# Softmax denominators of an attention layer: from a product with ones on TensorE to transpositions and sums on VectorE

## The chip, the cores and the metric

The kernel runs on one core of a Trainium2 chip. The metric is the time of one execution on the device in microseconds (us). A core has engines that run side by side, each with its own instruction queue, worked off in order: TensorE (PE in the profile; PEld is its weight load), VectorE (DVE), ScalarE (ACT), GpSimd (POOL) and SyncE (SP), which here issues most of the DMAs. They wait for one another through semaphores.

## What is computed

Four layers on a 512 x 64 x 64 image x, each of the form x = x + f(groupnorm(x)). Only the first one, an attention over the 4096 pixels, is touched:

```python
q, k, v = to_tokens(conv1x1(x, wq)), to_tokens(conv1x1(x, wk)), to_tokens(conv1x1(x, wv))
AA = jnp.sum(q * q, axis=-1)
sim = -(AA[:, :, None] + AA[:, None, :] - 2.0 * qk) * scale   # the key's norm is that of q
attn = jax.nn.softmax(sim, axis=-1)
out = jnp.einsum('bij,bjd->bid', attn, v)                     # 8 heads of 64
return conv1x1(out, wo)
```

Everything is float32. The softmax over the keys needs, for each query and head, the sum of the exponentials over all 4096 keys. That sum, its reciprocal and the multiplication with it are the subject of the change.

## The kernel before

The attention (`_attention_pairs`, lines 548 to 935) works on pairs of heads, 4 pairs, and for each pair on 8 blocks of 512 queries. x, K, V, and O stay in SBUF; the list QO holds Q of a pair and, after the division, its output O, in the same place.

For each pair, `project` (line 680) computes Q and K, and for pairs 0 and 2 also V of two pairs, by Strassen-Winograd's scheme of seven products p1 to p7 instead of eight. VectorE makes differences of X (tiles diff, line 463) and sums of weights (w_sum, line 450), TensorE makes the products (lines 467 and 535), and ScalarE and VectorE take them out of PSUM (kept, lines 509, 513, 740, 758, 760). The products are made in the order p1, p5, p2, p7, p6, p3, p4. The weights for the pair come by SyncE (line 696) and are scaled on GpSimd (line 404).

Then the blocks. A block has 32 steps t of 128 keys. In step t TensorE makes the scores of 128 keys and 512 queries for both heads (line 822, four products on quarters of 64 x 64 of its array), ScalarE takes the exponential (line 830, tile pt, 128 x 1024: keys on partitions, two heads of 512 queries side by side), and, two steps later, TensorE multiplies with V (line 842, two accumulators av in PSUM) and VectorE adds pt into acc (line 909). There are five pt buffers. At the end of a block, acc holds for each query 128 partial sums, one in each partition; they are still to be added over the partitions. The two av are added into avs (lines 914 and 919).

`close` (line 849) does the rest for a block, three steps into the next block (`t == AHEAD + 1`): two products with a matrix of ones sum acc over the partitions, and leave each sum on all 64 partitions of its head; VectorE inverts it (512 columns on 128 partitions), multiplies avs with it and makes two steps of a running check, `good`, that all sums lie within limits. A PSUM buffer is taken for it from the three that the scores use (tag "s"):

```python
for h in range(2):
    nc.tensor.matmul(ps[h * D : (h + 1) * D, :], ones, acc[:, ts(h, BLK)], start=True, stop=True)
rd = p3.tile([P, BLK], FP, tag="row", name="rd")
nc.vector.reciprocal(rd, ps)
nc.vector.tensor_mul(QO[pair][:, ts(b, BLK)], av, rd)
```

Of the 32 closings, 28 lie inside a block; those of block 7 of pairs 0 to 2 lie in the next pair's projection, after p5; the last lies among the last output products. In pair 3, `output` (line 864) follows each block from the second on: four chunks of four products with wo (line 869), added to X (line 873), with statistics for the next layer (line 877). At the end `good` is reduced to one number, okay, which every engine loads (line 947) for a branch (line 948): if a sum were out of its limits, a general version of the attention would run instead.

A scheduler orders the instructions of each engine by what they depend on and by the program's order; what is marked with `keep_in_program_order` stays in that order, the rest may move.

Of the kernel before, what the change touches and what calls it, by code (L numbers as in the profile page):

```python
# [10 lines left out]
FP = mybir.dt.float32  # L11
# [150 lines left out]
@with_exitstack  # L162
def trunk_kernel(ctx: ExitStack, tc: tile.TileContext, a: dict, out: bass.AP):
    nc = tc.nc

    base = ctx.enter_context(tc.tile_pool(name="base", bufs=1))
    small = ctx.enter_context(tc.tile_pool(name="small", bufs=1))


    X = base.tile([P, NC, N], FP, tag="X", name="X")  # L170
    def load_x(chunks, engines):
        for b in range(NB):
            for c, eng in zip(chunks, engines):
                eng.dma_start(out=X[:, c, ts(b, BLK)], in_=a["x"][c, :, ts(b, BLK)])

    load_x((0, 1), (nc.sync, nc.scalar))

    vec = base.tile([P, NVEC], FP, tag="vec", name="vec")
    nc.gpsimd.dma_start(out=vec, in_=a["vecs"])

    def vcol(name, i):
        at, n = _VEC_AT[name]
        return vec[:, at + i : at + i + 1]

    def vall(name):
        at, n = _VEC_AT[name]
        return vec[:, at : at + n]

    ident = base.tile([P, P], FP, tag="ident", name="ident")
    make_identity(nc, ident)  # L190

    gmask = base.tile([P, P], FP, tag="gmask", name="gmask")
    nc.gpsimd.memset(gmask, 1.0 / GROUP)
    for cm, step, first in ((1, -GROUP, 0), (-1, GROUP, GROUP - 1)):
        nc.gpsimd.affine_select(
            out=gmask,
            in_=gmask,
            compare_op=ALU.is_ge,
            fill=0.0,
            base=first,  # L200
            pattern=[[step, P // GROUP], [0, GROUP]],
            channel_multiplier=cm,
        )

    neg2 = base.tile([D, 1], FP, tag="neg2", name="neg2")
    nc.vector.memset(neg2, -2.0)

    def new_stats():
        return small.tile([P, NC, NB, 6], FP, tag="stats", name="stats")

    centered = _Centered(tc, small)

    dram = ctx.enter_context(tc.tile_pool(name="dram", bufs=1, space=bass.MemoryType.DRAM))
    F = [dram.tile([P, FORM.planes, FORM.plane], FP, tag=f"F{i}", name=f"F{i}") for i in range(NDW)]
    F3 = [
        dram.tile([P, FORM3.planes, FORM3.plane], FP, tag=f"G{i}", name=f"G{i}")
        for i in range(NQKV)
    ]
    Z = dram.tile([NB, BLK], FP, tag="Z", name="Z")

    stats, mv = _attention(
        tc, a, X, ident, gmask, neg2, small, new_stats, centered,
        lambda: load_x((2, 3), (nc.sync, nc.sync)),
    )

    stats, norm = _gated_convs(tc, a, X, vcol, vall, gmask, small, new_stats, centered, stats, mv, F)
    _linear_attention(tc, a, X, vcol, vall, ident, gmask, small, centered, stats, norm, F3, Z, out)

# [316 lines left out]
SUM_LOW, SUM_HIGH = 1e-20, 1e30  # L545


def _attention_pairs(tc, a, X, QO, gmask, small, centered, stats, mv, okay, load_rest):

# [16 lines left out]
    with tc.tile_pool(name="att1", bufs=1) as p1, tc.tile_pool(  # L568
# [95 lines left out]
        nc.vector.memset(halves, 0.0)  # L664
        nc.vector.memset(halves[0:D, 0:1], -2.0)
        nc.vector.memset(halves[D:P, 1:2], -2.0)
        ones = p1.tile([P, D], FP, tag="ones", name="ones")
        nc.vector.memset(ones, 1.0)
        good = p1.tile([P, BLK], FP, tag="good", name="good")
        nc.vector.memset(good, 1.0)  # L670
        K = p1.tile([P, N], FP, tag="K", name="K")
        V = p1.tile([P, N], FP, tag="V", name="V")
# [4 lines left out]

            return V if pair % 2 else QO[NC - 1]

        def project(pair, meanwhile=None):  # L680


            if pair == 0:
# [78 lines left out]
            late, psa = [], []  # L762
            if pair == 0:
                taken(1, 0, NC)
            pieces = differences(0)
            for k in range(NB // 2):
                after = iter(())
                for g, (wa, wb, ws, sums) in enumerate(made):
                    values = g + 1 < len(made)
                    dst = [home(pair), home(pair + 1)] if values else [Q, K]  # L770
                    steps = (turned if values else seven).steps(
                        wa, wb, ws, diff, view(k), bank, keep,
                        lambda m, n, ps, more: put(dst[m], 2 * k + n, ps, more),
                        p1_kept=begun.get((k, values)) if pair == 0 else None,
                    )
                    for n, step in enumerate(steps):
                        if n == 0:
                            next(sums, None)
                            next(pieces, None)
                            next(pieces, None)  # L780
                        if n == 1:
                            _all(sums)
                            _all(pieces)
                        step()
                        if n == 1 and meanwhile:
                            meanwhile()
                            meanwhile = None
                        if n == 3 and late:
                            late.pop()()
                        if not values and n == 2 and k + 1 < NB // 2:  # L790
                            pieces = differences(k + 1)
                        for _ in range(0 if values else {2: 2, 5: 4}.get(n, 0)):
                            next(pieces, None)
                if not psa:
                    psa.append(ps_s.tile([P, 2 * BLK], FP, tag="s", name="ps_a"))
                sq = ptp.tile([P, 2 * BLK], FP, tag="pt", name="sq")
                for n in range(2):
                    nc.scalar.activation(
                        sq[:, ts(n, BLK)], Q[:, ts(2 * k + n, BLK)], AF.Square
                    )  # L800
                late.append(lambda k=k, sq=sq: squares(k, sq))
# [44 lines left out]
                        start=(t == 0), stop=(t == NT - 1),  # L846
                    )

        def close(pair, b, av, acc):

            ps = ps_mm.tile([P, BLK], FP, tag="mm", name="ps_d")
            for h in range(2):
                nc.tensor.matmul(
                    ps[h * D : (h + 1) * D, :], ones, acc[:, ts(h, BLK)], start=True, stop=True
                )
            rd = p3.tile([P, BLK], FP, tag="row", name="rd")
            nc.vector.reciprocal(rd, ps)
            nc.vector.tensor_mul(QO[pair][:, ts(b, BLK)], av, rd)
            nc.vector.scalar_tensor_tensor(
                good, rd, 1.0 / SUM_HIGH, good, ALU.is_ge, ALU.mult  # L860
            )
            nc.vector.scalar_tensor_tensor(good, rd, 1.0 / SUM_LOW, good, ALU.is_le, ALU.mult)

        def output(b, chunks):
            cols = ts(b, BLK)
            for o in chunks:
# [4 lines left out]
                    )  # L871
                xs = X[:, o, cols]
                add = nc.vector.scalar_tensor_tensor(xs, ps, gain_out, xs, ALU.mult, ALU.add)
                if (b, o) == (NB - 1, 0):
                    past(mybir.EngineType.PE, mm)
                    past(mybir.EngineType.Pool, nc.gpsimd.memset(none, 0.0))
# [2 lines left out]
                    _aggregate(nc, mv, stats, o)  # L879

        for pair in range(HEADS // 2):
            project(pair, pair and (lambda: close(*done)))
            if pair == HEADS // 2 - 1:

                w = p1.tile([P, 3, NC, P], FP, tag="wqkv", name="wo")
                wo = [w[:, i] for i in range(3)] + [p1.tile([P, NC, P], FP, tag="wo", name="wo")]
                for o in range(NC):
                    ins = nc.sync.dma_start(out=wo[o], in_=a["L0_wo"][:, :, ts(o, P)])
                past(mybir.EngineType.SP, ins)
            done = None  # L890
            for b in range(NB):
                av = [
# [1 line left out]
                ]  # L894
                acc = p2.tile([P, 2 * BLK], FP, tag="acc", name="acc")
                pts = {}
                for t in range(NT + AHEAD):
                    if t < NT:
                        pts[t] = scores(pair, b, t)
                    if t == AHEAD + 1 and done is not None:  # L900
                        close(*done)
                    if t >= AHEAD:
                        u = t - AHEAD
                        pt = pts.pop(u)
# [16 lines left out]
                if pair == HEADS // 2 - 1 and 0 < b < NB - 1:  # L921
                    output(b - 1, range(NC))
            if pair == HEADS // 2 - 1:
                output(NB - 2, range(2))
                close(*done)
        output(NB - 2, range(2, NC))
        output(NB - 1, range(NC))


        one = p1.tile([P, 1], FP, tag="one", name="one")  # L930
        nc.vector.tensor_reduce(one, good, AX.X, ALU.min)
        ps = ps_mm.tile([P, BLK], FP, tag="mm", name="ps_ok")
        nc.tensor.matmul(ps[0:1, 0:1], one, ones[:, 0:1], start=True, stop=True)
        nc.vector.tensor_scalar(okay, ps[0:1, 0:1], float(P), None, ALU.is_ge)


def _attention(tc, a, X, ident, gmask, neg2, small, new_stats, centered, load_rest):

    nc = tc.nc
    gain_out = 1.0 / math.sqrt(C)  # L940
# [2 lines left out]
    okay = small.tile([1, 1], mybir.dt.int32, tag="okay", name="okay")  # L943
    stats = new_stats()
    mv = small.tile([P, NC, 2], FP, tag="mv", name="mv")
    _attention_pairs(tc, a, X, O, gmask, small, centered, stats, mv, okay, load_rest)
    found = nc.values_load(okay[0:1, 0:1])
    with tc.If(found < 1, label="general"):

# [1254 lines left out]
```

## Time and profile before

| What | Value |
|---|---|
| time, median of 3 runs | 3821.49 us (3817.75 to 3822.82) |
| the profiled execution's own time | 3822.72 us |
| its span in the profile | 3821.0 us |
| granted TensorE clock, mean | 0.996 |
| attention, first scores to last output product | 128.6 to 2243.4 us |
| weight loads (PEld) | 1658.8 us (43%) |
| the longest item by line on GpSimd and DMA | none near the span: GpSimd 4% busy, DMA about 1 GB/s for most of attention |

A busy time counts each moment once in which an engine works. Matmul records overlap each other, so the mean length of one (0.59 us) is longer than the pace at which they follow: eight of 64*64, four at a time, follow each other at 0.86 us. A float32 product appears as two records. In a line of groups, the numbers after the bar are busy time in us and the mean of one in ns; after the second bar is the idle time of the engine ahead of these instructions and what ended it. Idle time of VectorE behind ScalarE, and of ScalarE behind TensorE, means that TensorE sets the pace.

In the list of waits, the places where an engine waits for closing's results are few: weight loads for the scores wait 10.9 us in 28 times for rd, and one ScalarE copy in a projection waits 9.0 us for the multiplication with it.

### The profile page before, as it was taken

Reading aid. Unit: us, or ns where it says so; the run is one execution under the profiler, and the core shown is the slowest. Engines: PE = TensorE matmul, PEld = TensorE weight load, DVE = VectorE, ACT = ScalarE, POOL = GpSimd, SP = SyncE. Lnnn points to the kernel's source line nnn. Section 1 sums busy time; section 2 is a strip of 40 time slices with the busy share of each in tenths; the row PEclk is TensorE's granted clock in tenths of the full one; section 3 lists DMA queues with packets and bytes.
Section 4 is the critical chain, followed back from the end, with each engine's and each line's share of the span. In section 5 each row is a group of like instructions: output and inputs, shape, how many; then the busy total and the mean of one; then the engine's idle time right before and its main releaser. Section 6 shows DMA issues by size and latency. Waiting matters only on the chain. (4 is left out here: it accounts for less than half of the span.)

```text
span 3821.0 us, 81661 instructions
## 1 busy us (share of the span) xinstructions
PE 3753.6 (98%) x35298; PEld 1658.8 (43%) x35298; DVE 2693.8 (70%) x3261; ACT 2063.6 (54%) x2989; POOL 138.5 (4%) x117
## 2 busy tenths in 40 slices
PE   7999999999999999999999999999999999999999
PEld 5633334333364333343333334554444544455543
DVE  6677777777765777776766757766677677665537
ACT  2577774777735777746665645663246632354210
POOL 1000000000000000000000000000000000122122
PEclk9999999999999999999999999999999999999999
DMA  2000000000000000000000015772056730463312
GB/s 100 9 1 1 1 1 9 1 1 1 1 1 9 1 1 1 1 9 1 1 1 1 1 50 174 195 202 77 13 158 194 201 100 27 150 183 100 97 56 91
DMA packets 178414, 212.92 MB, mean 56 GB/s; under 512 B 13032, under 2 KB 121832, under 8 KB 177920
## 3 DMA queue, kind: packets, MB, share of 16 engines
q1 hardware_dynamic: 152384, 150.56, 14.3%
q10 hardware_dynamic: 25632, 57.01, 4.1%
q8 instruction: 280, 4.59, 0.5%
q14 instruction: 86, 0.70, 0.1%
q0 software_dynamic: 32, 0.06, 0.0%
HBM read 147.81 MB, written 59.77 MB: 54 GB/s over the span
## 5 line engine op out<-in xcount | busy, mean ns | idle before, releaser
L830 ACT ACTIVATE pt<-ps_s,A 128x512 f32<-128x512 f32 x2048 | 1286.2, 687 | 534.8 <-PE ps_s L822 527.2
L909 DVE TENSOR_TENSOR acc<-acc,pt 128x1024 f32<-128x1024 f32 x960 | 1174.3, 1223 | 327.9 <-ACT pt L830 301.8
L822 PE MATMUL ps_s<-O,K 64*64 64x512 f32 x8192 | 1111.7, 589 | 0.0
L822 PEld LDWEIGHTS ps_s<-O,K 64*64 64x64 f32 x8192 | 334.5, 133 | 553.3 <-issue 307.0
L842 PE MATMUL av<-pt,O 64*64 64x512 f32 x4096 | 558.3, 590 | 0.9 <-ACT pt L830 0.9
L842 PE MATMUL av<-pt,V 64*64 64x512 f32 x4096 | 554.4, 590 | 0.0
L1083 ACT COPY S<-S 32x1295 f32<-32x1295 f32 (+1 forms) x272 | 341.4, 1256 | 212.8 <-DMA S<-F 107.4
L842 PEld LDWEIGHTS av<-pt,O 64*64 64x64 f32 x4096 | 171.6, 133 | 275.8 <-issue 254.5
L842 PEld LDWEIGHTS av<-pt,V 64*64 64x64 f32 x4096 | 168.3, 133 | 281.0 <-issue 270.3
L1010 PE MATMUL ps<-diff,w_sum 128*128 128x512 f32 x516 | 241.9, 601 | 3.7 <-DVE w_sum L450 2.3
L1010 PEld LDWEIGHTS ps_cv<-S,T 64*32 64x32 f32 x13824 | 193.5, 105 | 110.4 <-issue 73.2
L1010 PE MATMUL ps_cv<-S,T 64*32 64x128 f32 x13824 | 232.4, 273 | 4.8 <-DVE turned L1137 1.6
L1010 PE MATMUL ps<-h,w_out_L 128*128 128x512 f32 x512 | 229.6, 599 | 1.5 <-DVE X L1364 1.4
L463 DVE TENSOR_TENSOR diff<-X 128x512 f32<-128x512 f32 x200 | 133.8, 686 | 72.1 <-PE ps L1010 46.2
L1010 PE MATMUL ps<-X,w_in_L 128*128 128x512 f32 x304 | 148.2, 620 | 11.0 <-ACT kept L1286 5.5
L391 ACT ACTIVATE X<-X,gn_less 128x512 f32<-128x512 f32 x118 | 74.5, 709 | 153.2 <-DVE gn_less L127 153.2
L1010 PE MATMUL ps<-h,pw_L 128*128 128x512 f32 x320 | 144.9, 602 | 2.6 <-DVE h L1352 2.3
L1010 PEld LDWEIGHTS ps<-diff,w_sum 128*128 128x128 f32 x516 | 94.6, 190 | 117.2 <-issue 107.3
L1010 PEld LDWEIGHTS ps<-h,w_out_L 128*128 128x128 f32 x512 | 94.0, 190 | 118.3 <-issue 96.5
L463 DVE TENSOR_TENSOR diff<-X,diff 128x512 f32<-128x512 f32 x200 | 135.2, 686 | 12.8 <-PE ps L1010 11.3
L1137 DVE STREAM_TRANSPOSE h<-ps_cv 128x512 f32<-128x512 f32 x112 | 109.4, 1051 | 48.2 <-PE ps_cv L1010 47.9
L1010 PE MATMUL ps<-agg,w_proj 128*128 128x512 f32 x256 | 118.4, 602 | 0.0
(239 smaller groups left out, 3336.1 us busy)
## 6 DMA issues: line engine op xcount, KB each, us to landing
T<-in_L_T_dram SPq DMA_DIRECT2D x112, 384.0 KB, 4.2
F<-plane ACTq DMA_DIRECT2D x112, 324.0 KB, 3.8
S<-F SPq DMA_DIRECT2D x224, 162.0 KB, 4.7
S<-G SPq DMA_DIRECT2D x96, 153.0 KB, 4.2
G<-plane ACTq DMA_DIRECT2D x48, 289.0 KB, 2.4
row<-G SPq DMA_DIRECT2D x48, 272.0 KB, 3.4
T<-in_L_T_dram SPq DMA_DIRECT2D x48, 256.0 KB, 3.9
out_dram<-y SPq DMA_DIRECT2D x32, 256.0 KB, 2.0
```

The source lines that it names most:

```text
L391: return self.nc.scalar.activation(xs, xs, AF.Identity, bias=less)
L463: yield eng.tensor_tensor(t[j][c], a(c), b(c), ALU.subtract)
L822: nc.tensor.matmul(ps[ts(half, D), ts(h, BLK)], K[rows, t * P + half * D : t * P + (half + 1) * D], QO[pair][rows, cols], start=True, stop ...
L830: exp = nc.scalar.activation(pt[:, ts(h, BLK)], ps[:, ts(h, BLK)], AF.Exp, bias=A[:, t, h : h + 1])
L842: nc.tensor.matmul(av[half][rows, :], v[keys, t * P + h * D : t * P + (h + 1) * D], pt[keys, ts(h, BLK)], start=(t == 0), stop=(t == NT - 1),)
L909: add = nc.vector.tensor_add(acc, acc if u > 1 else first, pt)
L1010: self.tc.keep_in_program_order(self.nc.tensor.matmul(*args, **kw))
L1083: nc.scalar.copy(second, first)
L1137: nc.vector.transpose(out, src)
```

## The change

`close` is replaced by `closing`, which gives four pieces to be put at chosen places: turn, partial, whole and divide. The sum over the partitions is made by VectorE: acc is transposed in 32x32 blocks in place (turn); each row of 32 is summed, from 128x1024 to 128x32 (partial); the four groups of 32 partitions are brought together by three copies and summed, the 1024 sums, now 32x32, are inverted and transposed back, written to a DRAM tile R, and read back twice, each time one head's 512 values onto 64 partitions (whole); then avs is multiplied (divide). The check `good` shrinks to 32x32. In a block, the pieces stand at steps 3, 6, 9 and 20; in a projection, after its first, second, third and seventh product; at the end, the first three before the outputs of block 6, and the division before the last chunk of these. The reciprocals' tile rd leaves the pool that it shared with kept and avs. The sums of weights of pairs 1 to 3 are listed ahead of the projection. The hint for the branch on SyncE moves from the wo loads to the last but one closing. The last product, ps_ok, becomes a transposition and sums.

```diff
-        def close(pair, b, av, acc):
-
-            ps = ps_mm.tile([P, BLK], FP, tag="mm", name="ps_d")
-            for h in range(2):
-                nc.tensor.matmul(
-                    ps[h * D : (h + 1) * D, :], ones, acc[:, ts(h, BLK)], start=True, stop=True
-                )
-            rd = p3.tile([P, BLK], FP, tag="row", name="rd")
-            nc.vector.reciprocal(rd, ps)
-            nc.vector.tensor_mul(QO[pair][:, ts(b, BLK)], av, rd)
...
+        def closing(pair, b, avs, acc):
+
+            within = b < NB - 1 or pair == HEADS // 2 - 1
+            pin = tc.keep_in_program_order if within else lambda ins: ins
+            rd = p1.tile([P, BLK], FP, tag="rd", name="rd")
+            one, recip = (rd[0:32, P + 32 * i : P + 32 * (i + 1)] for i in range(2))
+
+            def turn():
+                pin(nc.vector.transpose(acc, acc))
+
+            def partial():
+                pin(
+                    nc.vector.tensor_reduce(
+                        rd[:, 0:32], acc.rearrange("p (t k) -> p t k", k=32), AX.X, ALU.add
+                    )
+                )
+
+            def whole():
+                for q in range(1, P // 32):
+                    pin(
+                        nc.vector.tensor_copy(rd[0:32, ts(q, 32)], rd[ts(q, 32), 0:32])
+                    )
+                nc.vector.tensor_reduce(
+                    one, rd[0:32, 0:P].rearrange("p (q t) -> p t q", t=32), AX.X, ALU.add
+                )
+                nc.vector.reciprocal(one, one)
+                nc.vector.transpose(recip, one)
+                nc.sync.dma_start(out=R, in_=recip)
+                nc.vector.scalar_tensor_tensor(
+                    good, one, 1.0 / SUM_HIGH, good, ALU.is_ge, ALU.mult
+                )
+                nc.vector.scalar_tensor_tensor(
+                    good, one, 1.0 / SUM_LOW, good, ALU.is_le, ALU.mult
+                )
+                for h in range(2):
+                    ins = nc.sync.dma_start(
+                        out=rd[ts(h, D), :],
+                        in_=bass.AP(R.tensor, R.offset + h * BLK, [[0, D], [1, BLK]]),
+                    )
+                if (pair, b) == (HEADS // 2 - 1, NB - 2):
+                    past(mybir.EngineType.SP, ins)
+
+            def divide():
+                pin(
+                    nc.vector.tensor_mul(QO[pair][:, ts(b, BLK)], avs, rd)
+                )
+
+            return [turn, partial, whole, divide]
```

Where the pieces are put, in the projection, in the blocks and at the end:

```diff
             late, psa = [], []
             if pair == 0:
                 taken(1, 0, NC)
+            else:
+                _all(made[0][3])
...
-                        if n == 1 and meanwhile:
-                            meanwhile()
-                            meanwhile = None
+                        if meanwhile and n in (0, 1, 2, 6):
+                            meanwhile.pop(0)()
...
+                pieces = dict(zip((3, 6, 9, 20), closing(*done) if done else ()))
                 for t in range(NT + AHEAD):
                     if t < NT:
                         pts[t] = scores(pair, b, t)
-                    if t == AHEAD + 1 and done is not None:
-                        close(*done)
+                    if t in pieces:
+                        pieces[t]()
...
             if pair == HEADS // 2 - 1:
-                output(NB - 2, range(2))
-                close(*done)
-        output(NB - 2, range(2, NC))
+                pieces = closing(*done)
+                for piece in pieces[:3]:
+                    piece()
+                output(NB - 2, range(NC - 1))
+                pieces[3]()
+                output(NB - 2, range(NC - 1, NC))
         output(NB - 1, range(NC))
...
-        one = p1.tile([P, 1], FP, tag="one", name="one")
-        nc.vector.tensor_reduce(one, good, AX.X, ALU.min)
-        ps = ps_mm.tile([P, BLK], FP, tag="mm", name="ps_ok")
-        nc.tensor.matmul(ps[0:1, 0:1], one, ones[:, 0:1], start=True, stop=True)
-        nc.vector.tensor_scalar(okay, ps[0:1, 0:1], float(P), None, ALU.is_ge)
+        one = p1.tile([32, 32], FP, tag="one", name="one")
+        nc.vector.memset(one, 0.0)
+        nc.vector.tensor_reduce(one[:, 0:1], good, AX.X, ALU.min)
+        nc.vector.transpose(one, one)
+        nc.vector.tensor_reduce(one[0:1, 0:1], one[0:1, :], AX.X, ALU.min)
+        nc.vector.tensor_copy(okay, one[0:1, 0:1])
```

## The prediction, made before the changed kernel ran

> **What bounds the kernel now.** I read the busy shares first, then the costliest groups, then the tile that the change removes, then the timeline around it. In the page of before:
>
> ```profile
> PE 3753.6 (98%) x35298; PEld 1658.8 (43%) x35298; DVE 2693.8 (70%) x3261; ACT 2063.6 (54%) x2989; POOL 138.5 (4%) x117
> ...
> L830 ACT ACTIVATE pt<-ps_s,A 128x512 f32<-128x512 f32 x2048 | 1286.2, 687 | 534.8 <-PE ps_s L822 527.2
> L909 DVE TENSOR_TENSOR acc<-acc,pt 128x1024 f32<-128x1024 f32 x960 | 1174.3, 1223 | 327.9 <-ACT pt L830 301.8
> L822 PE MATMUL ps_s<-O,K 64*64 64x512 f32 x8192 | 1111.7, 589 | 0.0
> ```
>
> TensorE has no idle time ahead of the score products. ScalarE waits for TensorE, and VectorE waits for ScalarE. So in attention a microsecond taken out of TensorE's queue is a microsecond off the span, as long as the other two keep up. The view of the tile ps_d shows what the change takes out:
>
> ```profile
> L853 PE MATMUL ps_d<-acc,ones x128: 592/618/643, 189.7 to 2222.1; 128*64 128x512 f32 x128
> L857 DVE RECIPROCAL rd<-ps_d x32: 3343/3351/3357, 191.3 to 2223.0; 128x512 f32<-128x512 f32 x32
> ```
>
> 128 records are 32 closings of four (two products, each in two passes). Durations overlap, so the cost must be read from the TensorE timeline, here in block 2 of pair 0 (start, length, instruction, count):
>
> ```profile
> 300.06 1.04 PE L842 MATMUL av<-pt,O 64*64 64x512 f32 x8
> 300.92 1.04 PE L822 MATMUL ps_s<-O,K 64*64 64x512 f32 x8
> 301.89 1.08 PE L853 MATMUL ps_d<-acc,ones 128*64 128x512 f32 x4
> 302.90 1.09 PE L842 MATMUL av<-pt,O 64*64 64x512 f32 x8
> 303.81 1.04 PE L822 MATMUL ps_s<-O,K 64*64 64x512 f32 x8
> 305.52 1.04 PE L822 MATMUL ps_s<-O,K 64*64 64x512 f32 x8
> ```
>
> One step t (scores and values) takes 305.52 − 303.81 = 1.717 us. The step with the closing takes 303.81 − 300.92 = 2.89 us. **A closing costs TensorE 1.17 us.** The closings of blocks 1 and 2 start at 245.78 and 301.89: 56.11 us = 32 x 1.717 + 1.17, so nothing else is hidden in a block. On VectorE the same closing looks like this:
>
> ```profile
> 303.52 3.35 DVE L857 RECIPROCAL rd<-ps_d 128x512 f32<-128x512 f32 x1
> 306.79 1.16 DVE L909 TENSOR_TENSOR acc<-acc,pt 128x1024 f32<-128x1024 f32 x1
> 307.86 0.68 DVE L858 TENSOR_TENSOR O<-avs,rd 128x512 f32<-128x512 f32 x1
> 308.46 0.69 DVE L859 SCALAR_TENSOR_TENSOR good<-rd,good 128x512 f32<-128x512 f32 x1
> 309.06 1.22 DVE L909 TENSOR_TENSOR acc<-acc,pt 128x1024 f32<-128x1024 f32 x1
> 310.20 0.69 DVE L862 SCALAR_TENSOR_TENSOR good<-rd,good 128x512 f32<-128x512 f32 x1
> 310.80 9.20 DVE L909 TENSOR_TENSOR acc<-acc,pt 128x1024 f32<-128x1024 f32 x7
> ```
>
> It is a burst of 3.35 + 0.68 + 2 x 0.69 = 5.4 us that VectorE makes good over the next seven or more additions, at 9.20 / 7 = 1.31 us each against 1.717 us per step. TensorE's timeline shows no gap behind it. So a lag of some 4 us on VectorE is absorbed (five pt buffers).
>
> [...]four records at the pace of the 64*64 products (0.86 us for eight in four tiles, thus two rounds of 0.43 us) make 0.86 us for two column tiles, and the trace has 1.17, so the switch to 128*64 and back costs about 0.3 us. [...]the trace has 1.23 us for one of 128x1024 in SBUF (L1143). [...]the trace has 3.35 us for 512 columns, 6.5 ns each. [...]A later stage of this kernel does the same spread through DRAM:
>
> ```profile
> 3697.42 0.63 SPq L1900 DMA_DIRECT2D Z<-rz  x1
> ...
> 3699.21 0.35 ACTq L1937 DMA_DIRECT2D rz_b<-Z  x1
> ```
>
> The write of rz is back after 1.79 us at most, and the view of Z gives a landing time of 3.2 to 4.5 us. I take 6 us for the round trip.
>
> **The change part by part.**
>
> *Inside blocks, 28 closings (7 a pair).* TensorE loses the four ps_d records: 28 x 1.17 = 32.8 us. Is something late instead? The values product of t=1 would start 1.1 us earlier, at 301.78 instead of 302.90. In the block before, ScalarE starts at 242.49 and does exponentials at 0.594 us each, so pt of t=1 is ready at 244.9, and the product would start at 245.67: 0.8 us of margin, and more at the next step, where it is 246.1 against 247.39. The PSUM buffer that ps_d held until the reciprocal was done is free too (28 waits of a weight load for rd, 10.9 us in all, none in TensorE's idle time), a small help.
>
> VectorE: out go 3.35 + 2 x 0.69 = 4.7 us. In come the transposition (1.23), a reduction of 128x1024 (128x512 takes 0.68 at L1756, and 512 more columns add 0.54, as between the additions of 512 and 1024 columns: 1.2), three copies of 32x32, a reduction, a reciprocal (0.2 + 32 x 6.5 ns = 0.4), a transposition and two threshold steps on 32x32. Small operations of 128x4 follow one another at 0.20 us in the normalisation after attention, so eight of them make about 1.8 us; bounds 1.2 and 3. Sum 4.2 us, the division unchanged. In the order of the changed kernel the transposition stands between avs and the first addition, where VectorE sits idle for 2.0 us, so it is free. The reduction comes after 3 additions, the small steps after 3 more, the division after 11 more. No burst exceeds 1.9 us, against 5.4 before: no stall. The division comes 11 x 1.717 = 18.9 us after the small steps, the spread needs 6: no wait. SyncE issues three DMAs a closing and has nothing else in a block; the weight loads stand behind the closing of the projection, and wait there for buffers that come free later anyway. ScalarE and GpSimd keep their instructions and order.
>
> *Three projections (closing of block 7 of a pair).* TensorE loses ps_d: 581.74 to 582.75 is 1.01 us and its neighbours take 1.81 and 1.82 instead of 1.72, so 1.2 us. But here VectorE is full (18.4 of 20 us from 580 to 600), and all pieces but the division now stand before the evictions instead of after them. I redid the queue of pair 1 by its order, 0.60 us per operation of 512 columns: the addition of the p7 product is done at 589.1 instead of 587.2, while p4, which writes its bank, could start at 588.6: 0.5 us late. The eviction of p3 ends at 592.7 and p5 of the next round can start at 592.5: 0.2. The DMAs start at 587.6 and land near 593.6, the division stands ready at 592.7: VectorE waits 0.9 us, and behind it stand the eviction that frees av0, wanted at 596, and the differences: no loss. So 1.2 − 0.7 for pairs 1 and 3 and about 0.8 for pair 2, whose queue has pauses: 1.8 us. Bounds: +3.6 with no stall, −9 if small steps cost 0.35 us and the landing takes 9.
>
> *The end.* ps_d between the output products (2221.56 to 2222.57) goes: 1.0 us. The closing chain of the last block is now 1.23 + 1.2 + 1.8 + 6 + 0.7 = 11 us from 2214.6; TensorE has four output chunks of 3.43 us, until 2228.2, before it needs the result. The division also waits for the third chunk's eviction, until 2225.5. It is covered by 2 us. The product ps_ok goes (0.19), and okay is known before the last chunks; VectorE's branch stays behind its last aggregation at 2245.3, so I take 0.2 us (0 to 1). Together 1.2. After the branch the instructions stand as before.
>
> **Sum:** 32.8 + 1.8 + 1.2 = 35.8 us. From the profiled execution's 3822.72 this gives 3786.9; the median of the runs, 3821.49, is 1.2 lower, so 3785.7, and I say 3786.
>
> **Rivals.**
> - *Projections lose.* VectorE is the bound there, and the early pieces delay evictions: −9 instead of +1.8, so 3822 − 25 = 3797. For it: 92% busy in that window. Against: the pauses from 600 on (14.9 of 25 us busy).
> - *A wait takes its place.* TensorE arrives 1.17 us earlier and finds exponentials missing, so blocks keep their length: only the 3 us outside remain, 3819. For it: ScalarE runs without a pause at a block's start. Against: the 0.8 us of margin, and 0.45 us of idle per step afterwards.
> - *The spread holds VectorE up (slower).* The division waits in VectorE's queue with the additions behind it, which free the pt buffers. It begins to cost when the round trip passes 17 us of cover plus 4 us of lag, at 21; it eats the gain at 21 + 36/28 = 22.3; at 24 us it is 28 x 3 − 36 = +48, so 3869. Against: 6 us for the same spread at Z, in a stage with more DMA traffic; attention moves about 1 GB/s.
> - *More than expected.* No stall in the projections and the branch 1 us earlier: 39, so 3782.
>
> **Numbers.** Forecast 0.74, projections 0.14, wait 0.05, slower 0.03, more 0.04. The range: from 3782 less the runs' own spread of some 3 us, 3779, to the projections' case with 1 us of it, 3798. A measurement of this kernel tells 0.2% (7.6 us) from no change: faster 0.74 + 0.14 + 0.04 = 0.92, same 0.05, slower 0.03.
>
> **What would show it.** ps_d gone; closings of neighbouring blocks 54.9 us apart instead of 56.1; TensorE's busy time down by some 34 us and no new idle time before ps_s or av; VectorE rows of 32 transpositions at 1.23 and 32 reductions near 1.2; no wait of the division for DMA inside blocks, about 1 us in the projections; TensorE unbroken through the last outputs. I am wrong if TensorE shows idle time for pt at the starts of blocks, or if the division's waits for the DMA reach back to the additions.

## The result and the profile after

| | before | after |
|---|---|---|
| time, median | 3820.05 us (3817.75 to 3822.82) | 3789.36 us (3786.49 to 3793.32) |
| ratio after / before, 95% interval | | 0.992 (0.9903 to 0.9937) |
| span of the profiled execution | 3821.0 us | 3788.3 us |
| its own time | 3822.72 us | 3791.26 us |
| attention: first scores to first product of the second layer | 2124.5 us | 2089.4 us |
| from there to the end | 1567.9 us | 1571.4 us |

The kernel is 30.7 us faster by the medians, where 35.8 were forecast. The measured time lies 3.4 us above the forecast 3786.0, inside the forecast range of 3779 to 3798. The last two rows already say where to look: attention became 35.1 us shorter, and the layers after it, which the change does not touch, became longer.

The first part and three groups of the page of after:

```profile
PE 3716.6 (98%) x35168; PEld 1795.2 (47%) x35168; DVE 2676.3 (71%) x3487; ACT 2061.1 (54%) x2989; POOL 135.6 (4%) x117
...
L830 ACT ACTIVATE pt<-ps_s,A 128x512 f32<-128x512 f32 x2048 | 1284.5, 686 | 504.3 <-PE ps_s L822 496.6
L822 PE MATMUL ps_s<-O,K 64*64 64x512 f32 x8192 | 1428.1, 589 | 0.0
L945 DVE TENSOR_TENSOR acc<-acc,pt 128x1024 f32<-128x1024 f32 x960 | 1175.3, 1224 | 333.5 <-ACT pt L830 309.1
```

TensorE has 130 records fewer (35298 − 35168: 128 of ps_d, 2 of ps_ok) and is busy 37.0 us less; the score products still wait for nothing, and the order of who waits for whom is as before. The busy time of the scores' own line rose from 1111.7 to 1428.1 us with the mean record unchanged at 589 ns. That is not slower work: records overlap, and the two profiles interleave scores and values differently. Such a sum over overlapping records can't be compared between two kernels; the distance between two closings can. In after the transpositions of neighbouring blocks, here the one below and the one at 240.65 further down, start 54.9 us apart, where it was 56.1 before. That is the forecast distance, and it is 32 steps of 1.717 us with nothing else.

```profile
185.71 1.24 DVE L857 STREAM_TRANSPOSE acc<-acc 128x1024 f32<-128x1024 f32 x1
```

The view of the tile rd in after (duration as minimum/median/maximum in ns, then first and last start):

```profile
L869 DVE COPY rd<-rd x96: 169/170/174, 196.7 to 2184.1; 32x32 f32<-32x32 f32 x96
...
L861 DVE TENSOR_REDUCE rd<-acc x32: 1208/1212/1220, 191.6 to 2182.4; 128x32 f32<-128x1024 f32 x32
L871 DVE TENSOR_REDUCE rd<-rd x32: 350/365/369, 197.3 to 2184.3; 32x32 f32<-32x128 f32 x32
L874 DVE RECIPROCAL rd<-rd x32: 333/341/342, 197.7 to 2184.7; 32x32 f32<-32x32 f32 x32
L875 DVE STREAM_TRANSPOSE rd<-rd x32: 185/199/200, 198.0 to 2185.0; 32x32 f32<-32x32 f32 x32
...
L893 DVE TENSOR_TENSOR O<-avs,rd x32: 671/682/693, 215.3 to 2191.5; 128x512 f32<-128x512 f32 x32
its engine sat idle before it (us, times) until:
  DMA rd<-R: 3.0, 2
```

Thirty-two of each, as forecast, at the forecast prices. The two last lines answer the main question about the new wait: of 32 divisions, two waited for the DMA, 3.0 us together; both lie in projections, none in a block.

VectorE in block 2 of pair 0, the timeline of after (start, length, instruction, count, and in brackets the idle time ahead):

```profile
240.65 1.24 DVE L857 STREAM_TRANSPOSE acc<-acc 128x1024 f32<-128x1024 f32 x1
242.78 1.23 DVE L945 TENSOR_TENSOR acc<-pt 128x1024 f32<-128x1024 f32 x1 [0.89 <-ACT pt L830]
...
246.58 1.21 DVE L861 TENSOR_REDUCE rd<-acc 128x32 f32<-128x1024 f32 x1
247.71 3.87 DVE L945 TENSOR_TENSOR acc<-acc,pt 128x1024 f32<-128x1024 f32 x3
251.61 0.54 DVE L869 COPY rd<-rd 32x32 f32<-32x32 f32 x3
...
258.79 1.23 DVE L945 TENSOR_TENSOR acc<-acc,pt 128x1024 f32<-128x1024 f32 x1 [0.21 <-ACT pt L830]
...
270.23 0.68 DVE L893 TENSOR_TENSOR O<-avs,rd 128x512 f32<-128x512 f32 x1
```

The transposition fits into a pause, as 0.89 us of idle time still follow it. The reduction and the small steps put VectorE behind; by 258.79 it has caught up, since it waits for ScalarE again. The division comes eleven additions later with no bracket: it waits for nothing.

### The profile page after: what moved, and what is told of

It reads as the page before. It is cut to its first block, busy times and chain, and to the rows that moved or that the text cites. A ratio compares the mean times of both kernels' runs of the same rounds, so it can differ in the third digit from the quotient of the medians.

```text
span 3788.3 us, 81698 instructions
## 1 busy us (share of the span) xinstructions
PE 3716.6 (98%) x35168; PEld 1795.2 (47%) x35168; DVE 2676.3 (71%) x3487; ACT 2061.1 (54%) x2989; POOL 135.6 (4%) x117
## 5 line engine op out<-in xcount | busy, mean ns | idle before, releaser
L822 PE MATMUL ps_s<-O,K 64*64 64x512 f32 x8192 | 1428.1, 589 | 0.0
L842 PE MATMUL av<-pt,O 64*64 64x512 f32 x4096 | 769.8, 589 | 0.9 <-ACT pt L830 0.9
L822 PEld LDWEIGHTS ps_s<-O,K 64*64 64x64 f32 x8192 | 454.2, 133 | 478.6 <-issue 350.3
L842 PE MATMUL av<-pt,V 64*64 64x512 f32 x4096 | 659.7, 589 | 0.0
L842 PEld LDWEIGHTS av<-pt,O 64*64 64x64 f32 x4096 | 257.9, 133 | 213.6 <-issue 129.4
L842 PEld LDWEIGHTS av<-pt,V 64*64 64x64 f32 x4096 | 204.6, 133 | 270.1 <-issue 256.2
L1050 PE MATMUL vkp<-kT,vT 128*128 128x512 f32 x256 | 115.4, 593 | 3.6 <-DVE vT L1809 2.8
```

Source lines behind the costliest of these rows:

```text
L822: nc.tensor.matmul(ps[ts(half, D), ts(h, BLK)], K[rows, t * P + half * D : t * P + (half + 1) * D], QO[pair][rows, cols], start=True, stop ...
L842: nc.tensor.matmul(av[half][rows, :], v[keys, t * P + h * D : t * P + (h + 1) * D], pt[keys, ts(h, BLK)], start=(t == 0), stop=(t == NT - 1),)
L1050: self.tc.keep_in_program_order(self.nc.tensor.matmul(*args, **kw))
```

## The experiments

All times are medians; each ratio is against the kernel before on the same chip. Attention and the rest are from the profiles, divided at the first product of the second layer; they are differences of starts read to a tenth of a microsecond, so 0.1 us means nothing.

| Kernel | time us | before us | ratio, 95% interval | attention us | rest us |
|---|---|---|---|---|---|
| ones_back | 3824.68 | 3823.3 | 1.0004 (0.9997 to 1.0011) | 2122.2 | 1576.9 |
| quarters | 3818.31 | 3823.3 | 0.999 (0.9981 to 0.9999) | 2116.7 | 1571.0 |
| no_sums | 3790.4 | 3823.3 | 0.991 (0.9894 to 0.9927) | 2087.0 | 1579.4 |
| no_recip | 3820.8 | 3819.72 | 1.0002 (0.9993 to 1.001) | 2124.4 | 1565.8 |
| divide_9 | 3788.77 | 3819.72 | 0.9918 (0.9902 to 0.9933) | 2091.4 | 1568.7 |
| whole_later | 3786.08 | 3819.72 | 0.9913 (0.99 to 0.9927) | 2087.0 | 1568.3 |
| after_again | 3789.9 | 3823.3 | 0.9911 (0.9894 to 0.9928) | 2089.4 | 1571.7 |
| r_in_z | 3794.33 | 3823.6 | 0.9921 (0.9908 to 0.9935) | 2089.4 | 1575.6 |
| before_r | 3822.65 | 3823.6 | 0.9998 (0.999 to 1.0006) | 2124.4 | 1569.8 |
| later_z | 3792.68 | 3823.6 | 0.992 (0.9906 to 0.9933) | 2087.0 | 1574.7 |
| late_okay | 3796.1 | 3823.8 | 0.9926 (0.9912 to 0.994) | 2090.0 | 1579.3 |
| before_again | 3822.65 | 3823.8 | 0.9998 (0.999 to 1.0007) | 2124.6 | 1564.3 |

The attention column repeats within 0.2 us between runs of the same attention (2124.4 to 2124.6; 2089.4 twice more), while the last column moves by several us. So attention is judged from the profiles, to tenths of a microsecond, and the rest only from groups of runs.

### Does the gain come from TensorE's queue?

**ones_back**: the changed kernel, with the two products put back into each block at their old place; nobody reads what they make.

```diff
                     if t in pieces:
                         pieces[t]()
+                    if t == AHEAD + 1 and done is not None:
+                        ps = ps_mm.tile([P, BLK], FP, tag="mm", name="ps_d")
+                        for h in range(2):
+                            nc.tensor.matmul(ps[h * D : (h + 1) * D, :], gmask[:, 0:D], done[3][:, ts(h, BLK)], start=True, stop=True)
```

> The changed kernel, with the two products with a 128x64 matrix put back on TensorE in the 28 closings inside blocks, at the same place as before the change; nothing reads their result (their weights are 64 columns of another matrix, and they read the already transposed acc). VectorE's new work stays. Theory A (the gain is the TensorE time of these products, 1.17 us each with the change of tiling mode): the changed kernel plus 28 x 1.17 = 33 us, so about 3822. Theory B (the gain is the PSUM buffer that was held, or VectorE's reciprocal): clearly less than 33, near 3800 if it is half of it.

TensorE's timeline of ones_back in block 2:

```profile
301.36 1.04 PE L822 MATMUL ps_s<-O,K 64*64 64x512 f32 x8
302.33 1.08 PE L941 MATMUL ps_d<-acc,gmask 128*64 128x512 f32 x4
303.33 1.09 PE L842 MATMUL av<-pt,O 64*64 64x512 f32 x8
304.24 1.04 PE L822 MATMUL ps_s<-O,K 64*64 64x512 f32 x8
```

From scores to scores, 304.24 − 301.36 = 2.88 us, against 1.72 in the next step (305.96 − 304.24). Attention is 2122.2 − 2089.4 = 32.8 us longer than in after, which is 28 x 1.17. The products are the whole gain inside the blocks, although VectorE works here exactly as in after.

**quarters**: the kernel before, with the sums made on quarters of 64 x 64 so that all products in a block have the form 64*64; two half sums result, which VectorE copies and adds.

```diff
-            ps = ps_mm.tile([P, BLK], FP, tag="mm", name="ps_d")
-            for h in range(2):
-                nc.tensor.matmul(ps[h * D : (h + 1) * D, :], ones, acc[:, ts(h, BLK)], start=True, stop=True)
+            ps = ps_s.tile([P, 2 * BLK], FP, tag="s", name="ps_d")
+            for half in range(2):
+                keys = slice(half * D, (half + 1) * D)
+                for h in range(2):
+                    nc.tensor.matmul(ps[h * D : (h + 1) * D, ts(half, BLK)], ones[keys, :], acc[keys, ts(h, BLK)], start=True, stop=True)
             rd = p3.tile([P, BLK], FP, tag="row", name="rd")
-            nc.vector.reciprocal(rd, ps)
+            nc.vector.tensor_copy(rd, ps[:, 0:BLK])
+            nc.vector.tensor_add(rd, rd, ps[:, BLK : 2 * BLK])
+            nc.vector.reciprocal(rd, rd)
```

> The kernel before, with its sum over the partitions made by four products on quarters of the array (64x64, as the scores and values) into two PSUM banks, which VectorE copies and adds (1.4 us more on VectorE per closing). No change of tiling mode is left in a block. Theory A (0.3 of the 1.17 us is the switch of mode and back): a closing costs TensorE 0.86 us, so 28 x 0.31 = 9 us faster than before, about 3811. Theory B (the 1.17 us are the products themselves, or a wait for the buffer): no change or slower, 3820 or more.

Three of the score groups in its timeline, the sums lying between the first two:

```profile
300.70 0.69 PE L822 MATMUL ps_s<-O,K 64*64 64x512 f32 x4
...
303.28 0.69 PE L822 MATMUL ps_s<-O,K 64*64 64x512 f32 x4
...
304.99 0.69 PE L822 MATMUL ps_s<-O,K 64*64 64x512 f32 x4
```

The step with the sums takes 2.58 us, the next one 1.71: the sums cost 0.87 us here instead of 1.17. Attention is 7.8 us shorter than before's, 7.8 / 28 = 0.28 us a closing. So the prediction's reading of 1.17 as 0.86 of work and 0.3 of the switch to 128*64 and back holds: without the switch, 0.3 us are gone. What TensorE does in these 0.3 us the traces do not show. Nearly a quarter of the gain was to be had without moving the sums to VectorE. The time fell by only 5.0 us where 9 were expected: attention gave about 1 us less, and the layers after it took longer.

### What does the sum on VectorE cost?

**no_sums**: the changed kernel without transposition, reductions, inversion, limits or DMAs; avs is multiplied by a constant, so the softmax's sums and its division are left out.

```diff
-            def turn(): ...
-            def partial(): ...
-            def whole(): ...
+            turn = partial = whole = nothing
...
-                    nc.vector.tensor_mul(QO[pair][:, ts(b, BLK)], avs, rd)
+                    nc.vector.tensor_mul(QO[pair][:, ts(b, BLK)], avs, unit)
```

> The changed kernel without turn, partial and whole: no sums, no reciprocal, no DMA; avs is multiplied with a constant, so the softmax's division is left out. Theory A (VectorE's new work is covered everywhere except for about 1 us in each of the projections of pairs 1 and 3): 2 us faster than the changed kernel up to the end of attention, time 3784 to 3791. Theory B (VectorE's new work costs something in blocks too): over 6 us faster.

Attention is 2087.0 us, 2.4 less than after's. This bounds what all of VectorE's and SyncE's new work can cost there: 2.4 us. A block with a closing takes 54.93 us here as in after, so none of it lies in those blocks. It lies in the projections of pairs 1 and 3 (next section).

**no_recip**: the kernel before with a copy in place of the 3.35 us reciprocal; the inversion is left out.

```diff
-            nc.vector.reciprocal(rd, ps)
+            nc.vector.tensor_copy(rd, ps)
```

> The kernel before, with its reciprocal of 3.35 us replaced by a copy of 0.7 us (the inversion is left out). The products with ones stay. Theory A (VectorE's work in a closing does not bound the kernel before): no change, 3817 to 3823. Theory B (part of the change's gain came from VectorE losing the big reciprocal, or from the PSUM buffer being free earlier): several us faster.

Attention stays at 2124.4 us. Such a copy takes 0.68 us (rd<-ps_d in quarters, median of 32) where the reciprocal took 3.35, so by this estimate it also frees the PSUM buffer 2.7 us sooner. Making VectorE's closing shorter is worth nothing by itself, so none of the gain comes from the small reciprocal, and none from a shorter hold on that buffer.

**divide_9**: the changed kernel, with the division right behind the spread at step 9 and the additions kept behind it, so that VectorE must wait out the DMAs.

```diff
+                if pieces:
+                    pieces[9] = lambda w=pieces[9], d=pieces.pop(20): (w(), d())
...
+                            tc.keep_in_program_order(add)
```

> The changed kernel, with the division right behind the small steps in a block, so that VectorE waits for the whole round trip through DRAM with all additions queued behind it: about 5 us of idle time, a burst of nearly 8 us with the small steps and the division. Theory A (as the prediction's slower rival priced it: 4 us of lag are absorbed, more goes to TensorE): 1 us per block, some 28 us slower than the changed kernel, about 3817. Theory B (five pt buffers and three PSUM buffers absorb more than that): no slower than the changed kernel. Either way, without the cover of eleven additions the wait for the DMA shows in the division's row.

VectorE's timeline of divide_9 in block 2:

```profile
253.30 0.18 DVE L880 SCALAR_TENSOR_TENSOR good<-rd,good 32x32 f32<-32x32 f32 x1
258.14 0.69 DVE L893 TENSOR_TENSOR O<-avs,rd 128x512 f32<-128x512 f32 x1 [4.67 <-DMA rd<-R]
258.75 19.83 DVE L947 TENSOR_TENSOR acc<-acc,pt 128x1024 f32<-128x1024 f32 x15
```

The wait is real: 4.67 us here, and the view of the tile rd sums it up:

```profile
  DMA rd<-R: 139.0, 30
```

VectorE stood idle for 139 us in 30 closings (28 in blocks, 2 in projections, as in after), and attention grew by 2.0 us (2091.4 against 2089.4). Measured from block to block, 1.5 of these lie at the projections of pairs 1 and 3 and 0.5 in the blocks of pair 2; all other blocks are as long as in after. VectorE makes no addition from 251.65 to 258.75, 7.1 us in a row, then does 15 at 1.32 us each against a step of 1.72 us, and TensorE hardly notices. The theory that priced 4 us of lag as the limit, and so expected about 28 us of loss, falls.

### The projections

**whole_later**: the changed kernel, with the small steps of the projections behind the fifth product instead of the third.

```diff
-                        if meanwhile and n in (0, 1, 2, 6):
+                        if meanwhile and n in (0, 1, 4, 6):
...
+            late = (lambda ins: ins) if within else tc.keep_in_program_order
...
-                    pin(
+                    (pin if within else late)(
                         nc.vector.tensor_copy(rd[0:32, ts(q, 32)], rd[ts(q, 32), 0:32])
```

> The changed kernel, with the small steps (whole) in the three projections moved behind the additions of the products p7 and p6, so that they don't hold up the addition that the product p4 waits for. Theory A (the wait of TensorE of 1.0 us before p4 in the projection of pair 1, and its like in pair 3, comes from the order on VectorE): these waits go, 1 to 2 us off the attention; the division then waits for its DMA for 1 to 3 us without holding TensorE. Too little for the times to tell, to be read from the timeline. Theory B (the wait moves on to the evictions behind the division): the attention is no shorter.

TensorE in pair 1's projection, after:

```profile
577.62 1.88 PE L468 MATMUL ps<-X,w_sum 128*128 128x512 f32 x4
580.49 1.96 PE L468 MATMUL ps<-diff,wqkv 128*128 128x512 f32 x4 [1.00 <-DVE kept L510]
```

The same products in whole_later:

```profile
579.18 1.88 PE L468 MATMUL ps<-X,w_sum 128*128 128x512 f32 x4
580.90 1.88 PE L468 MATMUL ps<-diff,wqkv 128*128 128x512 f32 x4
```

In after, p4 stands still for 1.00 us until VectorE's addition of p7 is done, which frees its bank. The view of TensorE's waits in after gives its total, two times (us in total, times, longest), one in pair 1 and one in pair 3:

```profile
PE ps L468 <- DVE kept L510: 2.0, 2, 1.0
```

In whole_later the bracket is gone and attention takes 2087.0 us: 2.4 us shorter, the same as with no sums at all. In exchange the division waits longer; VectorE's timeline of whole_later:

```profile
590.09 0.69 DVE L894 TENSOR_TENSOR O<-avs,rd 128x512 f32<-128x512 f32 x1 [1.86 <-DMA rd<-R]
```

It costs TensorE nothing there. whole_later is the best version found, by the length of attention; its ratio, 0.9913, can't be told from after's 0.992.

### The layers after attention

**after_again** is the changed kernel once more, to see whether the longer rest is a variation of one profile.

> The changed kernel once more, unchanged. Up to the first product of the second layer its profile was 36.1 us ahead of the kernel before, at the end only 32.7. Theory A (the last 3.4 us are variation from run to run in the later layers, whose instructions and order are the same): the lead at that product is 36 +- 1 us again, the lead at the end differs from 32.7 by a microsecond or more in either direction. Theory B (the change costs the later layers 3 us each time): 36 and 33 again. Time 3785 to 3793.

The longer rest came again: 1571.7 us. The medians agree: time less attention is 1.7 to 6.8 us longer than in the kernel before on the same chip for all nine kernels with the new attention, and −1.2 to 2.8 us for the four other runs with the old one. The order of instructions behind the branch is the same on all engines in both kernels, so something else differs. One place is a convolution in a later layer. The stretch around it, from VectorE's last sum of weights w_qkv to the first product with agg, takes 87.7 to 87.8 us in all five profiles of kernels with the old attention, and 89.3 to 92.2 in the nine with the new one. TensorE there, first in before, then in after:

```profile
3344.18 2.00 PE L1010 MATMUL ps_cv<-S,T 64*32 64x128 f32 x120 [1.12 <-DVE S L1081]
```

```profile
3309.31 3.80 PE L1050 MATMUL ps_cv<-S,T 64*32 64x128 f32 x120 [1.14 <-DVE S L1121]
```

The same 120 records after the same pause, 1.8 us longer. A table of stretches of half a microsecond in after (busy us and instructions of PE, PEld, DVE, ACT, POOL, then granted clock, DMA share, GB/s):

```profile
3309.00:3309.50 0.50, 0.19 (x16) 0.19 (x24) 0.50 (x2) 0.50 (x1) 0.00 (x0) 1.00 1.11 269
3309.50:3310.00 0.50, 0.50 (x32) 0.50 (x24) 0.45 (x1) 0.50 (x2) 0.00 (x0) 0.51 0.97 336
3310.00:3310.50 0.50, 0.50 (x36) 0.50 (x26) 0.00 (x0) 0.50 (x1) 0.00 (x0) 0.50 0.15 51
...
3312.00:3312.50 0.50, 0.50 (x18) 0.10 (x2) 0.01 (x1) 0.00 (x0) 0.00 (x0) 0.50 0.67 156
3312.50:3313.00 0.50, 0.50 (x8) 0.19 (x7) 0.50 (x1) 0.00 (x0) 0.00 (x0) 0.57 0.91 304
```

The granted clock falls to 0.50 for about 3.4 us and comes back. Why here and not in before, where the pauses are the same? In the profiles of before and after, the changes of clock inside the span lie at multiples of 3.413 us from one another, so time can be cut into windows of that length. In after, both pauses ahead of these products, 0.85 and 1.14 us, fall into one window; TensorE is busy for 1.42 of its 3.41 us, and the next window is at half clock. In before, with pauses of 0.87 and 1.12 us, a boundary cuts the first pause, both windows are busier (2.98 and 1.86 us), and the clock stays at 1.00. The table by these windows (length, TensorE's busy time and instructions, granted clock, DMA share, GB/s), first of after, then of before:

```profile
3306.10:3309.51 3.41, 1.42 (x26) 1.00 1.20 227
3309.51:3312.93 3.42, 3.42 (x120) 0.50 0.38 117
```

```profile
3338.78:3342.19 3.41, 2.98 (x7) 1.00 1.13 294
3342.19:3345.61 3.42, 1.86 (x108) 1.00 0.96 212
```

By my count over the 14 profiles, TensorE at this place is 42% busy in one window in eight of the nine kernels with the new attention, and half clock follows in each. In late_okay and in the five with the old one a boundary falls into the pauses or between them, no window is less than 51% busy, and the clock stays at 1.00. (late_okay's stretch is longer through another window at half clock, from 3281.9.)

How much of the longer rest is it? I added up the half clock from the second layer's first product to the end of the span. The five executions of kernels with the old attention (before, before_again, before_r, no_recip, quarters) have 11.2 to 25.1 us of it, mean 20.3; the nine with the new one 25.1 to 32.0, mean 27.9. TensorE is busy in 17.7 and 23.2 us of these. As an estimate, if half of the time is lost at half clock (above, the same 120 records took 3.80 us against 2.00), the 7.6 us more are worth at most 3.8 us, and 2.7 if only TensorE's busy time counts. The rest of the kernel has means of 1567.7 us (1564.3 to 1571.0) and 1574.0 (1568.3 to 1579.4): 6.3 us apart. So the clock is a part of it, and 2.5 to 3.6 us are not explained. Two causes were tried for the longer rest: where R lies in DRAM, and when the branch is resolved.

**r_in_z** and **before_r** test where R lies in DRAM: the first puts R into rows of a tile that existed before, the second adds R and a write to it to the kernel before.

```diff
-    R = dram.tile([32, 32], FP, tag="R", name="R")
+    R = Z[0:2, :].rearrange("r (a b) -> (r a) b", b=32)
```

```diff
     Z = dram.tile([NB, BLK], FP, tag="Z", name="Z")
+    R = dram.tile([32, 32], FP, tag="R", name="R")
+    nc.gpsimd.dma_start(out=R, in_=ident[0:32, 0:32])
```

> The changed kernel, with the reciprocals' 4 KB of DRAM laid into the rows of Z, a DRAM tile that the last layer uses only much later, so that the DRAM tiles stand as in the kernel before. The attention stays as in the changed kernel, 2089 us from the first scores to the first product of the second layer. Theory A (what the profiles of the changed kernel lose after attention, 3 to 4 us, is variation): the later layers take 1565 to 1580 us as before, the time stays at 3785 to 3793. Theory B (the new DRAM tile makes the later layers' DMAs slower): the later layers return to 1568 us or less, and the time falls to 3783 to 3787.

> The kernel before, with the 4 KB DRAM tile added and written once at the start by a DMA of GpSimd, nothing else. Theory A: the time of the kernel before, within 2 us. Theory B: 3 to 4 us slower than the kernel before in the same call, all of it after attention.

The rest is 1575.6 us with R in the old tile and 1569.8 with R added to the kernel before: each stays within its own group. So a new tile in DRAM is not the cause.

**later_z** is whole_later with r_in_z's line.

> Both edits that may help, together: the small steps behind the additions of p7 and p6 in the projections, and the reciprocals laid into Z. Theory A: 2 to 2.5 us off the changed kernel's attention, as with the first edit alone, 2087 us, and a time within 2 us of that run's ratio to the kernel before (0.9913). Theory B: 3 us more than that.

Attention is 2087.0 us again, the rest 1574.7: nothing is gained over whole_later.

**late_okay** makes okay depend on the last statistics, so that the branch is resolved as late as it was before:

```diff
-        nc.vector.tensor_copy(okay, one[0:1, 0:1])
+        nc.vector.scalar_tensor_tensor(
+            okay, mv[0:1, NC - 1, 0:1], 0.0, one[0:1, 0:1], ALU.mult, ALU.add
+        )
```

> The changed kernel, with okay made to depend on the last channel statistics (times zero), so that every engine learns of the branch as late as in the kernel before instead of some 20 us earlier. Theory C (the changed kernel's later layers take some 4 us longer than those of the kernel before because SyncE, ScalarE and GpSimd pass the branch at another moment): the later layers are back at 1566 to 1571 us, and the time falls to 3784 to 3787. Theory A (variation): later layers anywhere from 1565 to 1580 us. The end of attention itself: up to 1 us later than in the changed kernel.

The rest is 1579.3 us, no shorter, so the early branch is not the cause. **before_again** is the kernel before, run beside it.

> The kernel before, unchanged, for one more sample of its later layers. Theory A: 1565 to 1580 us after the first product of the second layer. Theory D (the changed kernel's later layers are really slower): 1566 to 1571 us, as in the four profiles of the kernel before and its variants so far. Attention 2124.5 us.

Its rest took 1564.3 us, the lowest of all, with the least half clock (11.2 us).

**What stays open** is why the two pauses share a window in eight of nine kernels with the new attention and in none of five with the old one, and what makes up the remainder of the 6.3 us. ones_back has the products back in TensorE, and no_sums has neither sums nor R's DMAs; both belong to the slower group (27.2 and 30.3 us at half clock), so neither the lighter load of TensorE in the blocks nor VectorE's new work is needed for it. What all nine share (the new tail of okay, the order in the projections, an instruction stream of another length) was not taken apart further.

## Why the prediction was right, and where it was off

- **Blocks, 28 x 1.17 = 32.8 us.** Exact: blocks became 56.1 − 54.9 us shorter each, and ones_back gives back 32.8 us of attention.
- **No stall in the blocks; the wait of the exponentials as a rival.** Right. no_sums leaves room for 2.4 us in all of attention; whole_later, which only removes the stalls of two projections, gains the same.
- **VectorE's prices.** Transposition 1.24 (1.23 was taken, from one of 128x1024 at L1143 in before), reduction 1.21 (1.2), the small steps from 251.61 to 253.45 = 1.84 us (1.8). The spread took 4.9 us in divide_9, from the write's issue at 253.22 to the division at 258.14 (6).
- **Projections, +1.8 us.** 1.2 us came. From block 7 of a pair to block 1 of the next, less the 1.17 us of the closing in block 7, the gain was 0, 1.2 and 0 us for pairs 1, 2 and 3, where 0.5, 0.8 and 0.5 were forecast. That the sum is off by only 0.6 is in part luck, as the parts err both ways. The place of the stall was forecast right, p4 waiting for the addition of p7, but at 0.5 us; it was 1.0, because the addition ended some 0.5 us later in VectorE's full queue than counted out. whole_later, with that stall gone, gains 1.2 in each of the three, the prediction's upper bound of 3.6. The rival in which the projections lose did not occur; half of its mechanism did.
- **The end, 1.2 us.** The lead over before grows from 34.9 us at the last products with V to 36.1 at the next layer's first statistics, both counted from the spans' starts: 1.2. (1.0 us of both leads arose ahead of the attention, where the first scores start at 127.6 instead of 128.6; over all runs that start varies from 127.4 to 129.1 in both groups.) TensorE ran unbroken through the last outputs, as its timeline in after shows:

```profile
2176.90 2.75 PE L842 MATMUL av<-pt,V 64*64 64x512 f32 x24
2179.59 27.73 PE L903 MATMUL ps_o<-O,wo 128*128 128x512 f32 x64
```

- **"After the branch the instructions stand as before."** This is the step that failed. The instructions do stand as before, and that was taken for the same time, a term of zero. Attention's 35.1 us are only 0.7 short of the forecast 35.8; the other 4.4 us that the medians' 30.7 lack were lost later. In the two profiles the lead shrank by 3.4 us, from 36.1 at the start of the second layer to 32.7 at the end of the span, and the groups' means are 6.3 us apart. More half clock accounts for at most 3.8 of these, by the sums above; the cause of the remainder is open.
- **The slower rival.** It began at a round trip of 17 us of cover and 4 us of lag. divide_9 takes the cover away and leaves 4.67 us of waiting behind a burst of small steps, and attention loses 2.0 us. Most blocks lose nothing by about 7 us without an addition, so the rival lies further off than it was placed.

## What to carry to other kernels

When one engine bounds a stage without idle time, the gain of work taken from it is read from the step with and without that work in its timeline (2.89 − 1.72 us), and other engines may take over far longer work if they have idle time in every step and buffers in between. In a full stretch such as a projection, even 1.8 us of small steps placed two products too early cost a stall of 1.0 us; there the place matters more than the work. Allow some microseconds for stages that the change leaves alone: identical instructions took 3 to 6 us longer here. And where TensorE pauses, look at the busy share of a whole window of its clock, here 3.413 us: in after, pauses of 0.85 and 1.14 us in one window were followed by half clock and products 1.8 us longer (3.80 against 2.00); in before, such pauses with a boundary inside the first were not.

## What the runs showed of the hardware

- TensorE's granted clock has the values 1.00 and 0.50 in the profiles of before and after, with 31.7 and 38.5 us of their spans at 0.50; its mean is 0.995 to 0.998 over all 14 profiles. Some of the half clock lies in the middle of busy stages: in after from 3309.51 to 3312.93, behind pauses of 0.85 and 1.14 us. I counted the windows of 3.413 us at full clock in before and after together. All 11 in which TensorE was busy for at most 45% were followed by half clock; of 6 between 45 and 55%, 2 were; of 83 between 55 and 99%, none. Of the 2093 that show as full (99% or more), 2 were followed by it, and these hold 32 and 28 products of a single column (128x1, ps_pb), which the profile counts as busy.
- With five pt buffers and 0.4 us of slack per addition (1.72 − 1.32), VectorE went 7.1 us without an addition in divide_9, with almost no loss on TensorE (0.5 us in 28 blocks).
- The write to R and the reads that depend on it were issued only 1.38 us apart in after (253.19 and 254.57), and the whole spread took about 5 us (divide_9) for 4 KB written and twice 128 KB read.
